# A graph network of two layers in f32 on one core: the second layer's bias put into PSUM by ScalarE ahead of the products instead of by constant products

## The chip, the cores and the metric

The kernel runs on one core of a Trainium2 chip. The metric is the device time of one execution in microseconds; the time before is the median of three runs. A core has TensorE (PE, which multiplies matrices and writes only to PSUM), VectorE (DVE), ScalarE (ACT), GpSimd (POOL), and SyncE (SP), whose queue issues most of the DMAs. Each engine works through its own instruction list in order, and waits on semaphores for the others.

## The reference

`x` has 32 batches of 512 rows (channels) and 1024 columns (nodes). `adj` is 512 by 512. Everything is f32.

```
def L0(x, wq, wk, wm, bm):                 # wm is adj
    q = einsum('c,bcn->bn', wq, x);  k = einsum('c,bcn->bn', wk, x)
    scores = q[:, None, :] + k[:, :, None]
    scores = where(scores > 0, scores, 0.01 * scores)
    att = softmax(scores, axis=-1)
    agg = einsum('bcn,bmn->bcm', x, att)
    return relu(einsum('oc,bcm->bom', wm, agg) + bm[None, :, None])

def L1(x, W, bias):                        # W is adj
    return einsum('bnf,nm->bmf', x, W) + bias      # bias: one value per column

x = layernorm(x + L0(x, wq, wk, adj, bm))          # over the 1024 columns
x = layernorm(x + L1(x, adj, bias))
```

## The kernel before, in words

**Layer 0.** A score depends only on the sum of one q and one k, so the softmax-weighted sums over the nodes can be had from nodes sorted by q and running sums. Per batch the kernel

- loads x (`ld`), forms q and k on PE (`pa`, copied by `pc`; turned by `co`, copied by `cc`), writes q to DRAM as a row (`qw`) and reads it back into all partitions (`ro`, the tile `qb`);
- finds each node's rank by q on DVE (`rk`, eight instructions of 128 by 1024) and the number of partners beyond the leaky unit's bend on ACT (`ct`, eight), closed by `re` and `ce`;
- forms z = adj times x per node on PE. Nodes of the first half come from plain products (`z`, four 128 by 512 tiles, copied by ACT, `zc`); those of the second half from Strassen's seven quarter products (`zU`, `zV`, `zY`, `z11`, `zZ`, `z12`, `z21`, with copies by ACT `zUc`, `zVc`, `zZc`, `zll` and sums on DVE `zup`, `zlr`; operands `x1` to `x4`). The first and the last batches take plain products for all;
- scatters the rows of z to DRAM in sorted order (`sc`, POOL's queue), loads them as a table (`sl`), weights them (`se` on ACT), runs prefix sums up (`u`) and down (`d`) on DVE, closes these across partitions with one-sided triangular products (`cu`, `cd` on PE; ACT's copies `uc`, `te`, `dc`; DVE's additions `tu`, `td`) and writes the table to DRAM (`tw`, and its last row `tl`);
- gathers each node's row (`g`, POOL's queue), forms the weights (`mw`), mixes (`ms` on ACT, `mx` on DVE), transposes back on PE (`t`), adds the residual (`r`, DVE), and normalises (`s0`, `rt`, `rce`, `n0` on ACT).

**Layer 1.** Per batch a product of 512 by 512 with 512 by 1024, again by Strassen's seven products, each in two row groups g = 0, 1 of 128 rows: `U`, `V`, `Y`, `21` gather in a bank `sum`, `11`, `Z`, `12` in a two-bank tile `pair`. adj with 1 added on its diagonal contains the residual. One product is two matmuls of 128 by 128 by 512. DVE makes the operands `t1` to `t4`; ACT copies partial sums out while the bank goes on gathering (`Uc`, `Vc`, `Zc`, `ll`), DVE adds (`up`, `lr`); then the second normalisation (`s1` on ACT, `ra`, `rb`, `r1` on POOL, `n` on ACT) and the store (`st`).

**The bias in layer 1.** Each bank of a sum, and the upper bank of each pair, begins with one row of constants in all its partitions: the sum with the bias of the first 512 columns, the pair with the second half's minus the first's, because Strassen's scheme adds the sum into both halves. A matmul of constants puts it there and opens the group in `quarter` (line 665 in the profile): a 128-row tile `bias_p` of bf16 whose first six rows hold the two halves' bias in three bf16 parts, and a broadcast column `first_0` or `first_10` that selects signs. `bias_parts` makes the rows once at the start.

**PSUM.** Eight banks: pool `p2` has two tiles of two banks (`pair`, the z pairs and the transposes of `t`), pool `p1` has four tiles of one bank under one tag, handed round by the pool: z tiles, `zsum`, `sum`, carries, q and k.

**Order.** The order of the work is written out by hand as lists of words: `head`, `loop` and `tail`. A word is an operation, a batch relative to the list's base, and indices; `emit` issues them in that order, so that each engine's list is the list's words for it in their order. In `loop` batch 0 is in ranking and z, batch -1 in its table, -2 in gathering and mixing, -3 in layer 1. `loop` is run for bases 14 to 18; head and tail write all other batches out.

Of the kernel before, what the change touches and what calls it, by code (L numbers as in the profile page):

```python
# [42 lines left out]
P = 128  # L43
# [6 lines left out]
def adj_resnorm_kernel(  # L50
# [25 lines left out]
    s4 = ctx.enter_context(tc.tile_pool(name="s4", bufs=4))  # L76
    dr = ctx.enter_context(tc.tile_pool(name="dr", bufs=1, space=bass.MemoryType.DRAM))
    p2 = ctx.enter_context(tc.tile_pool(name="p2", bufs=2, space=bass.MemoryType.PSUM))
    p1 = ctx.enter_context(tc.tile_pool(name="p1", bufs=4, space=bass.MemoryType.PSUM))
    ctx.enter_context(tc.manual_schedule())  # L80

# [10 lines left out]
    wqk = const.tile([P, CT, 32], F32, name="wqk")  # L92
# [7 lines left out]
    def adj_load(b):  # L100
        nc.sync.dma_start(out=adj_in, in_=adj.rearrange("(r p) c -> p r c", p=P))

    small = const.tile([P, 16], F32, name="small")
    nbm, eps, power = small[:, 0:4], small[:, 4:5], small[:, 5:9]
    own, spare, inner = small[0:6, 9:14], small[0:1, 14:15], small[:, 15:16]
    room = one.tile([P, NT, 2 * ZR], F32, tag="tab", name="bias_in")[0:6, :, 0:H]
    for h in range(2):
        nc.scalar.dma_start(
            out=room[3 - 3 * h : 6 - 3 * h, 0, :],
            in_=bias[h * H : (h + 1) * H].partition_broadcast(3),  # L110
        )
# [30 lines left out]
    zero = one.tile([P, ZR], F32, tag="end", name="zero")[0:1, :]  # L142
# [15 lines left out]
    bias_p = const.tile([P, H], BF16, name="bias_p")  # L158
    first = const.tile([P, 16], BF16, name="first")
    first_0, first_10 = first[:, 0:1].broadcast_to([P, P]), first[:, 1:2].broadcast_to([P, P])  # L160
    nc.vector.memset(bias_p, 0.0)
    nc.vector.memset(first, 0.0)

    def weights():
        t = p1.tile([P, C], F32, tag="m", name="rows_tp")[:, 0 : 3 * CT]
        nc.tensor.transpose(t, rows, ident[0 : 3 * CT, 0 : 3 * CT])
        nc.vector.tensor_copy(wqk[:, :, 0:2], t[:, 0 : 2 * CT].rearrange("p (r t) -> p t r", r=2))
        nc.vector.tensor_scalar(nbm, t[:, 2 * CT : 3 * CT], -1.0, None, ALU.mult)

    def adj_turn(b):  # L170
        for r in range(CT):
            t = p1.tile([P, CT, P], F32, tag="m", name=f"adj_tp_{r}")
            for c in range(CT):
                nc.tensor.transpose(t[:, c, :], adj_in[:, r, c * P : (c + 1) * P], ident)
            adj_ps.append(t)

    def adj_copy_odd(b):
        for r in range(1, CT, 2):
            nc.scalar.copy(adj_t[:, :, r * P : (r + 1) * P], adj_ps[r])

    def adj_copy_even(b):
        for r in range(0, CT, 2):
            nc.vector.tensor_copy(adj_t[:, :, r * P : (r + 1) * P], adj_ps[r])
        for r in range(CT):
# [16 lines left out]
    def bias_parts(b):  # L201


        i6 = ident[0:6, 0:6]
        nc.vector.tensor_tensor(own[:, 0:3], i6[:, 0:3], i6[:, 3:6], ALU.subtract)
        nc.vector.tensor_reduce(own[:, 3:4], i6[:, 3:6], axis=AX.X, op=ALU.add)
        nc.vector.tensor_scalar(own[:, 4:5], own[:, 3:4], -1.0, None, ALU.mult)
        nc.vector.tensor_copy(first[0:6, 0:1], own[:, 4:5])
        nc.vector.memset(first[0:6, 1:2], 1.0)
        rest, done = room[:, 0, :], room[:, 1, :]  # L210
        for i in range(3):
            part = one.tile([P, 2 * ZR], BF16, tag="end", name=f"bias_part_{i}")[0:6, 0:H]
            nc.vector.tensor_copy(part, rest)
            if i < 2:
                nc.vector.tensor_tensor(rest, rest, part, ALU.subtract)
            if i == 0:
                nc.vector.tensor_scalar(done, part, own[:, 0:1], None, ALU.mult)
            else:
                nc.vector.scalar_tensor_tensor(
                    done, part, own[:, i : i + 1], done, ALU.mult, ALU.add  # L220
                )
        nc.vector.tensor_copy(bias_p[0:6, :], done)
# [18 lines left out]
    def parts(b):  # L241

        s = st[b]
        s.ps = p1.tile([P, C], F32, tag="m", name=f"qk_ps_{b}")[:, 0:Q]
        for c in range(CT):
            for g in range(CT):
                nc.tensor.matmul(  # L247
                    s.ps[32 * g : 32 * g + 32, :], wqk[:, c, :],
# [8 lines left out]
    def cols(b):  # L257
        s = st[b]
        s.ps = p1.tile([P, C], F32, tag="m", name=f"qk_tp_{b}")[:, 0:Q]
# [25 lines left out]
    def top(b):  # L285
        s = st[b]
        settle(b)
        s.ntop = s4.tile([P, 2], F32, tag="top", name=f"top_{b}")
# [4 lines left out]
    def top_end(b):  # L293
# [3 lines left out]
        s.bd = s4.tile([P, 2, NT], F32, tag="bd", name=f"bd_{b}")  # L297
# [3 lines left out]
    def rank(b, j):  # L301
        s = st[b]
        if s.rank is None:
            s.rank = sp.tile([P, NT], F32, tag="rank", name=f"rank_{b}")
        if s.junk is None:
            s.junk = one.tile([P, 4 * ZR], U8, tag="end", name=f"junk_v_{b}")[:, 0:N]
# [11 lines left out]
    def count(b, j):  # L318
        s = st[b]
        if s.sign is None:  # L320
            s.sign = sp.tile([P, NT], F32, tag="sign", name=f"sign_{b}")
# [5 lines left out]
    def count_end(b):  # L327
        s = st[b]
        s.of = s4.tile([P, NT], U32, tag="of", name=f"of_{b}")
# [12 lines left out]
    def product(b, j):  # L342
        s, xt = st[b], xts[b]
        s.z[j] = p1.tile([P, C], F32, tag="m", name=f"z_ps_{b}_{j}")
# [57 lines left out]
    def zU(b):  # L402
        st[b].zsum = p1.tile([P, C], F32, tag="m", name=f"z_sum_ps_{b}")
# [55 lines left out]
    def sums_load(b, h):  # L459
# [4 lines left out]
        if s.tab is None:  # L464
            s.tab = one.tile([P, NT, 2 * ZR], F32, tag="tab", name=f"tab_{b}")
            s.zs = s.tab[:, :, ZR : 2 * ZR]
            s.ac = sp.tile([P, 2, NT], F32, tag="ac", name=f"ac_{b}")
# [14 lines left out]
    def up(b, j):  # L482
# [5 lines left out]
        if j == NT - 1:  # L488
            s.end = one.tile([P, ZR], F32, tag="end", name=f"end_{b}")
            s.up.append(s.end)  # L490
# [793 lines left out]
```

## Time and profile before

| | |
|---|---|
| median of three runs | 1941.6 us (1938.44 to 1947.02) |
| the profiled execution: its time, its span | 1942.71 us, 1940.9 us |
| mean granted clock of TensorE | 0.993 |
| busy: PE, DVE, ACT, POOL | 1887.8, 1704.6, 1483.5, 897.2 us |
| moved by DMA | 558 MB, 288 GB/s on average |
| line 665, constant products | 128 records, 48.4 us busy |

In the profile a line reads: source line, engine, operation, output tile <- input tiles, count, then busy time in all and the mean length in ns of one, then the time that the engine stood idle just before these instructions and what ended most of that. Matmul records overlap: a record runs until its last column has left the array, while the next has long begun. An f32 matmul appears as two records. A wait is put down to what came last.

### The profile page before, as it was taken

To read this page: it belongs to the slowest core of one execution; us is meant where nothing else is said; L and a number is where in the kernel's file an instruction comes from. 1 tells how busy PE (TensorE), PEld (TensorE's weight loads), DVE (VectorE), ACT (ScalarE), POOL (GpSimd) and SP (SyncE) were. 2 spreads that over 40 slices of the span, in tenths; PEclk is the share of its full clock that TensorE was granted. 3 is DMA by queue.
4 is the path that set the end of the run, shared out by engine and by line. 5 is a ranking of instruction groups with operands and counts; after the bars stand their busy time and mean duration, and the time that the engine had idled before them with its cause. 6 is when DMAs were issued, how large, how long until landed. Compare 5 with 4: busy or idle time off the path is not lost.

```text
span 1940.9 us, 23403 instructions
## 1 busy us (share of the span) xinstructions
PE 1887.8 (97%) x7073; PEld 1072.0 (55%) x7073; DVE 1704.6 (88%) x2746; ACT 1483.5 (76%) x2663; POOL 897.2 (46%) x1074
## 2 busy tenths in 40 slices
PE   7988999999999999999999999999999999999897
PEld 3654555555555555566555566555565555554443
DVE  6897899998899889989988989988998989889973
ACT  3566677878778777778787778787777787877786
POOL 5263435335434345454456454455443355445531
PEclk9999999999999999999999999999999999999899
DMA  6577788677888687877787887777888677887862
GB/s 250 197 290 271 286 309 339 253 294 282 313 310 315 252 309 270 331 307 291 290 306 280 317 311 304 277 299 286 308 312 310 262 291 300 308 320 279 331 245 95
DMA packets 147446, 558.05 MB, mean 288 GB/s; under 512 B 19653, under 2 KB 19793, under 8 KB 139129
## 3 DMA queue, kind: packets, MB, share of 16 engines
q1 hardware_dynamic: 89936, 354.40, 48.4%
q0 software_dynamic: 57344, 202.15, 27.6%
q8 instruction: 56, 0.92, 0.2%
q14 instruction: 70, 0.57, 0.1%
q10 hardware_dynamic: 40, 0.02, 0.0%
HBM read 287.08 MB, written 269.42 MB: 287 GB/s over the span
## 4 chain that ended last, share of the span: by engine, by line
PE 78%; DMA 8%; DVE 7%; issue 2%; ACT 2%; POOL 2%; SPq 0%; POOLq 0%; DVEq 0%; ACTq 0%
PE z_ps L346 19%; PE sum_ps L667 18%; PE pair_ps L667 10%; PE z_sum_ps L390 9%; PE z_pair_ps L390 7%; PE pair_ps L702 5%; PE agg_ps L609 4%; DMA table<-tab 3%; PE qk_ps L247 3%; DMA tab<-sorted_z 2%; DVE tab L538 2%; PE carry_ps_True L509 1%; PE carry_ps_False L509 1%; DMA x<-in_x_dram 1%; DMA sorted_z<-zt,to 1%
## 5 line engine op out<-in xcount | busy, mean ns | idle before, releaser
L563 POOL DMA_INDIRECT got<-table,of x256 | 302.3, 1181 | 568.8 <-DMA table<-tab 260.6
L346 PE MATMUL z_ps<-adj_t,x 128*128 128x512 f32 x1088 | 486.9, 594 | 1.4 <-DVE qkc L267 1.1
L451 POOL DMA_INDIRECT sorted_z<-zt,to x256 | 314.0, 1226 | 176.7 <-issue 73.9
L308 DVE SCALAR_TENSOR_TENSOR junk_v<-qb,qkc,tie 128x1024 uint8<-128x1024 f32 x256 | 329.8, 1288 | 10.0 <-DMA qb<-q_row 6.4
L346 PEld LDWEIGHTS z_ps<-adj_t,x 128*128 128x128 f32 x1088 | 202.3, 190 | 225.5 <-issue 212.4
L323 ACT ACTIVATE junk_s<-qb,qkc 128x1024 uint8<-128x1024 f32 x256 | 293.4, 1146 | 19.7 <-DMA qb<-q_row 14.3
L667 PE MATMUL sum_ps<-zt,S 128*128 128x512 f32 x512 | 236.1, 593 | 3.1 <-DVE zt L651 1.4
L585 ACT ACTIVATE got<-got,w 128x512 f32<-128x512 f32 x256 | 172.6, 718 | 42.2 <-DVE w L580 41.8
L590 DVE SCALAR_TENSOR_TENSOR got<-got,w 128x512 f32<-128x512 f32 x256 | 185.6, 746 | 12.0 <-ACT got L585 11.8
L491 DVE SCALAR_TENSOR_TENSOR tab<-tab,ac 128x514 f32<-128x514 f32 x192 | 144.6, 753 | 49.8 <-ACT tab L486 29.2
L617 DVE SCALAR_TENSOR_TENSOR x<-agg_ps,small,x 128x1024 f32<-128x1024 f32 x128 | 163.1, 1280 | 23.9 <-PE agg_ps L609 23.6
L600 ACT ACTIVATE junk<-g,tv 128x1024 uint8<-128x1024 f32 x128 | 146.9, 1148 | 32.9 <-DVE g L722 26.4
L501 DVE SCALAR_TENSOR_TENSOR tab<-tab,ac 128x513 f32<-128x513 f32 x224 | 167.5, 748 | 2.6 <-ACT tab L499 1.9
L667 PEld LDWEIGHTS sum_ps<-zt,S 128*128 128x128 f32 x512 | 96.5, 190 | 121.6 <-issue 105.8
L753 POOL TENSOR_SCALAR tv<-tv 128x1 f32<-128x1 f32 x124 | 53.1, 428 | 238.5 <-ACT junk L600 230.5
L774 ACT ACTIVATE g<-g,nb,tv 128x1024 f32<-128x1024 f32 x124 | 151.0, 1237 | 7.3 <-POOL nb L764 7.2
L600 ACT ACTIVATE junk<-x,tv 128x1024 uint8<-128x1024 f32 x128 | 146.9, 1148 | 12.2 <-DVE x L617 9.9
L538 DVE TENSOR_TENSOR tab<-tab,carry 128x2052 f32<-128x2052 f32 x64 | 146.2, 2291 | 4.7 <-ACT carry L516 4.7
L635 ACT ACTIVATE x<-x,tv 128x1024 f32<-128x1024 f32 x128 | 139.3, 1141 | 0.5
L609 PEld LDWEIGHTS agg_ps<-ident,got 128*128 128x128 f32 x1024 | 116.4, 141 | 36.2 <-issue 24.9
L609 PE MATMUL agg_ps<-ident,got 128*128 128x128 f32 x1024 | 129.4, 274 | 2.7 <-DVE g L722 2.0
L667 PE MATMUL sum_ps<-x,adj 128*128 128x512 f32 x256 | 123.3, 605 | 7.4 <-ACT x L635 7.4
(144 smaller groups left out, 3281.5 us busy)
## 6 DMA issues: line engine op xcount, KB each, us to landing
table<-tab SPq DMA_DIRECT2D x64, 2056.0 KB
tab<-sorted_z SPq DMA_DIRECT2D x64, 1028.0 KB
x<-in_x_dram SPq DMA_DIRECT2D x128, 512.0 KB
out_dram<-g SPq DMA_DIRECT2D x128, 512.0 KB
qb<-q_row SPq DMA_DIRECT2D x32, 512.0 KB
sorted_z<-zt,to POOLq DMA_INDIRECT x256, 5.0
got<-table,of POOLq DMA_INDIRECT x256, 8.0
adj_in<-in_adj_dram SPq DMA_DIRECT2D x1, 1024.0 KB
```

The source lines that it names most:

```text
L308: nc.vector.scalar_tensor_tensor(s.junk, s.qb, s.q[:, j : j + 1], tie[:, at : at + N], ALU.subtract, ALU.is_gt, accum_out=s.rank[:, j : j ...
L323: nc.scalar.activation(junk, s.qb, AF.Sign, bias=s.k[:, j : j + 1], accum_out=s.sign[:, j : j + 1])
L346: nc.tensor.matmul(s.z[j], xt[:, c, j * P : (j + 1) * P], adj_t[:, c, :], start=(c == 0), stop=(c == CT - 1),)
L390: nc.tensor.matmul(ps, a[:, i, k * P : (k + 1) * P], v[:, i, :], start=start and i == 0 and (k == 0 or bank == 1), stop=(i == 1), skip_gro ...
L451: nc.gpsimd.indirect_dma_start(out=sorted_z[b % 2][:, :], out_offset=bass.IndirectOffsetOnAxis(ap=s.to[:, j : j + 1], axis=0), in_=zt[:, j ...
L538: nc.vector.tensor_tensor(v, v, c, ALU.add)
L563: nc.gpsimd.indirect_dma_start(out=s.got[:, j, :], out_offset=None, in_=table[b % 2][:, :], in_offset=bass.IndirectOffsetOnAxis(ap=s.of[:, ...
L585: nc.scalar.activation(down, down, AF.Copy, scale=s.w[:, 1, j : j + 1])
L590: nc.vector.scalar_tensor_tensor(up, up, s.w[:, 0, j : j + 1], down, ALU.mult, ALU.add)
L600: nc.scalar.activation(junk, t, AF.Square, bias=v[0][:, i : i + 1], scale=-float(N), accum_out=v[1][:, i : i + 1],)
L609: nc.tensor.transpose(s.agg[o][:, j * P : (j + 1) * P], s.got[:, j, o * P : (o + 1) * P], ident)
L667: nc.tensor.matmul(ps, a[:, k, g * P : (g + 1) * P], v[:, k, :], start=False, stop=(k == 1), skip_group_check=first is None,)
```

## The change

ScalarE writes the bias into the banks. A tile `seed` holds the 1024 bias values in all partitions (one DMA on SP's queue at the start, and one DVE subtraction that makes the second half relative to the first). `sum_seed` (word `Us`) takes a bank and copies the first half of `seed` into it; `pair_seed` (word `Zs`) copies the second half into the pair's upper bank; the products of `U` and `Z` then add. [...]

`seed` takes 4 KB of each partition. To make room, `rank`, `sign`, `ac`, the first normalisation's statistics and the mixing weights go to single buffers, three others from four to three; the tag `end` is dropped: the last prefix row is written into `tab`'s first row, the totals into `qb`'s buffer, `junk_v` into that of `part`. All three lists are new; `loop` is run for bases 15 to 18.

```diff
+    idle, held, filled = [0, 1, 2, 3], {}, [False] * 4
+    def bank(name, key, keep=False, whole=True, shape=None):
+        want = [i for i in idle if filled[i] == keep] or idle
+        i = want[0]
+        idle.remove(i)
+        held.setdefault(key, []).append(i)
+        t = p1.tile(shape or [P, C], F32, tag=f"m{i}", name=name)
+        was, filled[i] = filled[i], whole
+        return (t, was) if keep else t
+    def release(key):
+        for i in held.pop(key, []):
+            idle.append(i)
...
     def adj_load(b):
         nc.sync.dma_start(out=adj_in, in_=adj.rearrange("(r p) c -> p r c", p=P))
+        nc.sync.dma_start(out=seed, in_=bias.partition_broadcast(P))
...
     def bias_parts(b):
-        nc.vector.tensor_copy(first[0:6, 0:1], own[:, 4:5])
-        nc.vector.memset(first[0:6, 1:2], 1.0)
-        rest, done = room[:, 0, :], room[:, 1, :]
-        for i in range(3):
-            part = one.tile([P, 2 * ZR], BF16, tag="end", name=f"bias_part_{i}")[0:6, 0:H]
-            nc.vector.tensor_copy(part, rest)
...
-        nc.vector.tensor_copy(bias_p[0:6, :], done)
+        nc.vector.tensor_tensor(seed[:, H:N], seed[:, H:N], seed[:, 0:H], ALU.subtract)
...
         if j == NT - 1:
-            s.end = one.tile([P, ZR], F32, tag="end", name=f"end_{b}")
-            s.up.append(s.end)
+            s.up.append(s.tab[:, 0, 0:ZR])
...
     def table_up_end(b):
-        carry_copy([t[0:1, :] for t in st[b].cup], st[b].end[0:1, :])
+        st[b].end = one.tile([P, N], F32, tag="qb", name=f"total_{b}")[0:1, 0:ZR]
+        carry_copy([t[0:1, :] for t in st[b].cup], st[b].end)
...
         for j in range(NT):
-            nc.tensor.transpose(
-                s.agg[o][:, j * P : (j + 1) * P], s.got[:, j, o * P : (o + 1) * P], ident
+            nc.tensor.matmul(
+                s.agg[o][:, j * P : (j + 1) * P], s.got[:, j, o * P : (o + 1) * P], ident,
+                is_transpose=True, start=(j % 4 == 0), stop=True, skip_group_check=True,
             )
...
-    def quarter(ps, a, v, g, first=None):
-        if first is not None:
-            nc.tensor.matmul(ps, first, bias_p, start=True, stop=False)
+    def quarter(ps, a, v, g):
         for k in range(2):
             nc.tensor.matmul(
                 ps, a[:, k, g * P : (g + 1) * P], v[:, k, :], start=False, stop=(k == 1),
...
+    def sum_seed(b, g):
+        s = st[b]
+        s.sum[g], ready = bank(f"sum_ps_{b}_{g}", f"s.{b}.{g}", keep=True)
+        if not ready:
+            nc.tensor.matmul(
+                s.sum[g], none[:, 0:1].broadcast_to([P, P]), none[:, 0:1].broadcast_to([P, H]),
+                start=True, stop=True,
             )
+        nc.scalar.copy(s.sum[g], seed[:, 0:H])
+    def pair_seed(b, g):
+        nc.scalar.copy(pair(b, g)[:, H:N], seed[:, H:N])
...
     def U(b, g):
-        s.sum[g] = p1.tile([P, C], F32, tag="m", name=f"sum_ps_{b}_{g}")
-        quarter(s.sum[g], A11, quarters(b)[0], g, first_0)
+        quarter(s.sum[g], A11, quarters(b)[0], g)
...
     def Z(b, g):
-        quarter(st[b].pair[g][:, H:N], S1, st[b].T1, g, first_10)
+        quarter(st[b].pair[g][:, H:N], S1, st[b].T1, g)
```

A bank is released in `emit` after the word that reads it last (`pc`, `cc`, `zc`, `zll`, `uc` and `te`, `dc`, `ll`). The part of `loop` around the first products of layer 1, before and after:

```
before:
    n0.-3.1 z12.0 g.-2.2 zlr.0 n0.-3.2 t1.-3 U.-3.0 g.-2.5 n0.-3.3 re.0 zup.0 se.-1.0 ct.0.1
    z21.0 sc.0.4 u.-1.0 sc.0.5 11.-3.1 Uc.-3.0 u.-1.1 ct.0.4 t2.-3 g.-2.7 zll.0 11.-3.0 u.-1.2
    se.-1.1 u.-1.3 g.-2.6 V.-3.0 u.-1.4 mw.-2.0 g.-2.4 u.-1.5 ms.-2.2 U.-3.1 Vc.-3.0 u.-1.6
after:
    rk.0.0 sl.-1.1 g.-2.2 zZ.0 rk.0.7 zVc.0 ct.0.6 g.-2.1 tp.-1 zY.0 rk.0.2 zZc.0 Us.-3.0 g.-2.3
    n0.-3.0 z12.0 zlr.0 n0.-3.3 g.-2.5 rk.0.6 se.-1.0 U.-3.0 n0.-3.2 t1.-3 u.-1.0 re.0 zup.0
    z21.0 Uc.-3.0 ct.0.1 u.-1.1 sc.0.4 t2.-3 11.-3.1 zll.0 ct.0.4 u.-1.2 sc.0.5 11.-3.0 Zs.-3.0
    u.-1.3 Us.-3.1 Zs.-3.1 g.-2.4 se.-1.1 V.-3.0 u.-1.4 g.-2.7 mw.-2.0 U.-3.1 u.-1.5 ms.-2.2
```

## The prediction

> **What bounds the kernel now.** I read the page's first part, then the PE groups with shapes kept apart, then the stretch table, then PE's timeline across one batch, and last the waits.
>
> ```profile
> span 1940.9 us, 23403 instructions
> PE 1887.8 (97%) x7073; PEld 1072.0 (55%) x7073; DVE 1704.6 (88%) x2746; ACT 1483.5 (76%) x2663; POOL 897.2 (46%) x1074
> ```
>
> TensorE (PE) is busy for all but 53.1 us. Where those lie is in the stretch table (columns: width, then busy time of PE, PEld, DVE, ACT, POOL, each with its count, then granted clock, DMA share, GB/s):
>
> ```profile
> 0.00:60.00 60.00, 49.45 (x220) 26.13 (x221) 39.33 (x79) 24.42 (x42) 27.69 (x38) 0.97 0.65 227
> ...
> 120.00:180.00 60.00, 48.19 (x164) 26.73 (x163) 49.84 (x83) 37.34 (x71) 28.99 (x33) 0.97 0.65 249
> ...
> 778.00:836.00 58.00, 58.00 (x223) 33.51 (x222) 52.34 (x86) 46.24 (x84) 28.42 (x33) 1.00 0.80 309
> ...
> 1770.00:1830.00 60.00, 55.59 (x170) 26.99 (x168) 55.23 (x87) 45.54 (x85) 29.52 (x30) 0.97 0.92 354
> 1830.00:1890.00 60.00, 51.49 (x148) 24.83 (x148) 49.87 (x81) 51.35 (x88) 29.55 (x35) 0.94 0.70 264
> 1890.00:1940.90 50.90, 38.71 (x111) 18.11 (x109) 20.25 (x34) 32.16 (x57) 5.77 (x16) 0.91 0.23 93
> ```
>
> The start, the fill (120 to 180) and the last 170 us hold 10.6 + 11.8 + 4.4 + 8.5 + 12.2 = 47.5 us of the idle time. In the middle PE is busy without a gap, at full clock. A busy PE need not be at its peak, so I read the repeat length from the chain of waits instead:
>
> ```profile
> 776.35 6.87 PE z_ps L346 x16
> ...
> 834.60 6.87 PE z_ps L346 x16
> ```
>
> The line comes again at 892.83 and 951.07: one batch takes 58.24 us, and the same 16 records take 6.87 us each time: 0.429 us for a 512-column pass, two passes for one f32 product. In a batch DVE needs 52.4 and ACT 46.2 us. So PE sets the pace, DVE is 10% away, ACT 20%.
>
> **The change, part by part.**
>
> *The constant products go.* Their groups:
>
> ```profile
> L665 PE MATMUL pair_ps<-bias_p,first 128*128 128x512 bf16 x64 | 24.2, 379 | 0.0
> L665 PE MATMUL sum_ps<-bias_p,first 128*128 128x512 bf16 x64 | 24.2, 379 | 0.0
> ```
>
> 128 of them, 48.4 us busy. That is not what they cost, because a record's 379 ns contains the pipeline's run-out beneath the next product. The timeline of PE gives start to start:
>
> ```profile
> 806.54 0.38 PE L665 MATMUL sum_ps<-bias_p,first 128*128 128x512 bf16 x1
> 806.75 1.88 PE L667 MATMUL sum_ps<-x,adj 128*128 128x512 f32 x4
> ```
>
> 806.54 to 806.75, and in the chain of waits 0.21 to 0.22 apiece: 0.214 us, half a 0.429 pass. [...] The row is this kernel's own stream, so 27.4. Their weight loads (128 of 98 ns) lie under the pass before and give nothing.
>
> *Some come back.* [...] So 4 x 0.214 = 0.9 us returns. [...]
>
> *What was free already.* Four constant products stand right before a wait of PE and were hidden in it: at 142.48 us (then 4.41 idle), 1796.15 (1.65), 1843.10 (0.45), 1872.13 (0.92). Again 0.9 us that isn't saved.
>
> Net from PE: 27.4 - 0.9 - 0.9 = **25.6 us**, 0.83 a batch: the period should go from 58.24 to 57.4.
>
> *ScalarE's 128 seeds.* No row copies SBUF to PSUM. Nearest by shape are
>
> ```profile
> L585 ACT ACTIVATE got<-got,w 128x512 f32<-128x512 f32 x256 | 172.6, 718 | 42.2 <-DVE w L580 41.8
> ...
> L687 ACT COPY g<-sum_ps 128x512 f32<-128x512 f32 x64 | 36.5, 575 | 24.7 <-PE sum_ps L667 24.6
> ```
>
> SBUF to SBUF with a scale operand 172.6/256 = 0.67 us, from PSUM 36.5/64 = 0.57. I take 0.6: 77 us in all (73 to 86), 2.4 a batch, so ACT goes from 46.2 to 48.6 of 57.4. I put it on the path at nothing in the middle, for this reason (waits of 720 to 1340 us, ten and a half batches: total, times, longest):
>
> ```profile
> ACT zt L352 <- PE z_ps L346: 15.3, 10, 1.8
> ...
> ACT zt L426 <- PE z_pair_ps L390: 12.4, 11, 1.1
> ACT g L693 <- PE sum_ps L667: 12.3, 11, 2.9
> ACT g L687 <- PE sum_ps L667: 11.6, 7, 4.5
> ```
>
> It is ACT that waits for PE, 51.6 us in these four rows, 4.8 a batch; PE has no entry of like size the other way. What is queued behind the seeds: `Us.-3.0` stands before `n0.-3.0`, for which its own product `U.-3.0` waits, and delays it by 0.6. The tightest place is the second sum. Its bank is zsum's, free after `zll.0`. From the end of `z21.0` PE has `11.1`, `11.0` and `V.0`, three of 1.72, 5.2 us, before `U.1`. ACT in that time has the rest of `Uc.0` and `ct.0.1` (0.2 us, since both take 0.57 + 1.27 from the end of `U.0` and `z21.0` runs 1.72), `zll` 0.57, `ct.0.4` 1.27, `Zs.0` and `Us.1` 1.2: 3.2 us. Two us to spare. At the batch's turn `zUc` now follows `ct.7` and two `s0` (3.8 us) and `zV` waits for it; under it lie `z11` 1.72 and `z.0.0` 3.44, again 5.2 against 4.4.
>
> *Other moves, one answer: nothing in the middle.* The last prefix row goes into `tab` where the carry is written later; the totals share `qb`'s buffer, so `qb`'s load also waits for the 2 KB `table_last`. The lists put that write ahead of `qw`, whose own landing `qb` already waited for (issued 828.80, `qb` 830.42: 1.6 us covers it). `junk_v` shares `part` with the carry, behind `td` on DVE's own queue. `rank`, `sign`, `ac`, `r` get one buffer, whose last readers stand earlier in the lists. `ce` moves back to just ahead of the next batch's first `ct`; the gathers that read it on POOL's queue come two batches later, and POOL gets and loses nothing but one queue position of some gathers. At worst the first `ct` waits for a landing; uncovered that is 0 to 1.6 us a batch, below nothing excluded, and I take 0.
>
> *The two ends.* Gone from DVE at the start is the run of bias parts, 37.64 to 43.09 us, for one 128x512 subtraction (0.69, by x_sums L373): 4.8 us of DVE, but PE was busy then. The 512 KB seed load stands on SP ahead of the first `qb`, while that `qb` moves ahead of `ld.1`'s four loads (4 x 0.43 us of issue); the first landing took 7.45 us. Between -5 and +3 for the start. In the tail ACT is at 51.4 of 60 and gets about 3 x 2.4 us more: 0 to +7. The new lists may win or lose waits at both ends that no row prices; I allow 10 us each way and take 0 for all.
>
> *Sum.* The profiled execution took 1942.7 us around its span of 1940.9, 1.1 over the median of 1941.6. 1942.7 - 25.6 = 1917.1; against the median, **1916 us**, 1.3% less.
>
> **The rivals.**
>
> *A: the mechanism as summed, 1916*, 1905 to 1929 with the ends. For it: no gap on PE in the middle, and ACT ahead of PE. 0.74.
>
> *B: ScalarE comes late to a seed, slower.* Place: `Zs.0` and `Us.1` behind `zll.0`, with `U.1` waiting. If ACT arrives 2 us late there, from a late table row at `se` (ACT waited 57.8 us for that load in 27 places, up to 7.8, but only 2.4 in the middle stretch) or from DVE's mixing weights (30.6 us in the middle), both seeds show: 1.2 us of PE idle a batch, 32 x 1.2 = 38, so 1916 + 38 = 1954. It decides from 0.8 us of wait a batch, where it eats the gain. Against it: the 2 us of room and the 4.8 us of waiting for PE that can absorb it. 0.11.
>
> *C: the period stays.* The round from table write to gather, or DVE, holds 58.2 us and the seeds only make PE wait: 1941.6 + 0, say 1939 with the ends. For it: DVE at 52.4, DMA at 80%. Against: PE shows no gap in the middle, and would if another round were the longer one. 0.09.
>
> [...] 0.06, together with losses of this size at the ends.
>
> **How the numbers follow.** About 0.5% (9.7 us, so below 1932 or above 1951) is what a measurement of this kernel can tell from no change. Faster: A's 0.74 and most of D, 0.79. Same: C and the rest, 0.10. Slower: B, 0.11. The predicted time is A's. The range 1904 to 1937 holds A and D and leaves out B, C's most, and a luckier start below.
>
> **What would show it.** Right: no L665 row but 4; copies `sum_ps<-seed` and `pair_ps<-seed`, 128 together, at 0.57 to 0.67 us; the same z_ps line in the chain recurring every 57.4 us; PE busy without gap in the middle stretches; ACT near 1560 us busy, its waits for PE smaller. Wrong: PE rows `sum_ps <- ACT sum_ps` or `z_sum_ps <- ACT zt` with about 1 us each batch (B); a period of 58.2 with PE gaps (C); idle at the ends more than 10 us above 47.5.

## The result: 0.8% slower, and the profile after

The changed kernel takes 1957.18 us (median of five runs, 1956.14 to 1961.67) against 1942.06 for the kernel before (five runs, 1938.44 to 1947.02): a ratio of 1.0084 (1.007 to 1.0098). The prediction had 1916 us and a 0.11 chance of slower. The profiled execution took 1956.8 us around a span of 1955.1. From its page, then its groups:

```profile
span 1955.1 us, 23300 instructions
PE 1876.8 (96%) x6949; PEld 1058.8 (54%) x6949; DVE 1697.8 (87%) x2732; ACT 1543.5 (79%) x2791; POOL 870.5 (45%) x1073
```

```profile
L669 ACT COPY sum_ps<-seed 128x512 f32<-128x512 f32 x64 | 37.6, 587 | 5.8 <-PE sum_ps L665 5.7
L678 ACT COPY pair_ps<-seed 128x512 f32<-128x512 f32 x64 | 37.4, 585 | 25.4 <-PE pair_ps L708 24.8 <-DVE zt L426 0.6
L665 PE MATMUL sum_ps<-none 128*128 128x512 bf16 x4 | 1.8, 442 | 0.0
```

The change does what it says. The constant products are gone but for four zero products (those of `none`, which `sum_seed` runs ahead of a seed where `filled` does not note the bank that `bank` hands it), as forecast, and ScalarE makes 128 seeds of 0.585 us. PE's busy time fell by 11 us, yet its idle time rose from 53.1 to 78.3. The repeat length in the middle, from the chain of waits:

```profile
764.02 6.87 PE sum_ps L656 x16
821.63 6.87 PE sum_ps L656 x16
```

57.61 us, where 58.24 stood before and 57.4 was forecast. The loop got faster. The rest is in the stretch table (same columns as before) and in PE's waits (what waits <- what ended the wait: total, times, longest):

```profile
0.00:60.00 60.00, 49.29 (x219) 25.32 (x220) 36.17 (x66) 25.87 (x44) 30.01 (x38) 0.97 0.67 240
...
120.00:180.00 60.00, 44.80 (x130) 24.37 (x129) 47.13 (x79) 37.83 (x69) 24.62 (x32) 0.86 0.67 262
778.00:836.00 58.00, 58.00 (x222) 33.20 (x221) 52.34 (x86) 48.75 (x89) 27.30 (x36) 1.00 0.80 300
...
1770.00:1830.00 60.00, 53.55 (x142) 25.36 (x142) 48.69 (x71) 45.88 (x86) 22.08 (x31) 0.96 0.84 321
1830.00:1890.00 60.00, 48.47 (x146) 23.49 (x147) 48.91 (x77) 50.73 (x89) 30.37 (x37) 0.94 0.75 274
1890.00:1955.10 65.10, 50.22 (x137) 22.32 (x135) 31.22 (x55) 44.88 (x80) 9.70 (x20) 0.95 0.27 108
```

```profile
PE sum_ps L656 <- ACT sum_ps L669: 10.6, 10, 2.6
...
PE pair_ps L708 <- ACT x L627: 5.8, 3, 4.5
PE carry_ps_False L501 <- ACT part L248: 5.5, 1, 5.5
PE carry_ps_True L501 <- DVE tab L483: 4.5, 1, 4.5
PE agg_ps L600 <- DVE x L609: 4.5, 1, 4.5
```

Two of these waits have a counterpart of the same size in the kernel before:

```profile
PE sum_ps L667 <- ACT x L635: 7.4, 4, 4.4
...
PE carry_ps_True L509 <- DVE end L491: 4.2, 1, 4.2
```

The stretches at the start, in the fill and at the end now hold 10.7 + 15.2 + 6.5 + 11.5 + 14.9 = 58.8 us of PE's idle time, 11.3 more than before. The middle row has no gap. Apart from the first row, the waits shown are mostly long single ones. That first row, ten waits, is PE waiting for seeds of the sums; for seeds of the pairs it waited 1.0 and 0.7 us in two further rows.

**One measure for all the runs.** Busy time hides what a lower clock costs (in the last section the same four records are busy for 2.05 us at a granted clock of 0.50 and for 1.03 without such a period), so I charge every PE record with the distance to the next that its kind shows in an unbroken run (0.429 us for 512 columns of f32, where a record lasts 0.594; 0.215 for bf16, where it lasts 0.379; 1.864 for the 32 records of q and k, and so on), and call the rest of the distance lost. The count runs from PE's first record to its last. Stretches begin and end where the products of a batch's `cu` start. Kernels with "no bias" are explained below.

| | work of PE | lost to batch 2's `cu` | lost from there to batch 28's | lost from there on | lost in all |
|---|---|---|---|---|---|
| before | 1858.2 | 25.0 | 16.3 | 23.0 | 64.3 |
| after | 1831.6 | 35.9 | 30.5 | 39.5 | 105.9 |
| old lists, no bias (e3) | 1830.8 | 25.3 | 16.6 | 24.3 | 66.2 |
| old lists, seeds in gaps (e8) | 1831.8 | 25.3 | 25.5 | 33.7 | 84.5 |
| new lists, no bias (e6) | 1830.8 | 33.2 | 22.4 | 35.2 | 90.8 |
| new head, old rest, no bias (e7) | 1830.8 | 33.2 | 17.1 | 23.3 | 73.6 |
| old head and loop, new tail, no bias (e10) | 1830.8 | 24.4 | 19.9 | 37.2 | 81.5 |

So the change took 26.6 us of work from PE, close to the forecast, and made it lose 41.6 us more. The experiments ask which of the change's three other parts did that: the seeds on ScalarE (theory S), the order of the new lists (L), or the buffers that were joined to make room for the seed (B).

### The profile page after: what moved, and what is told of

Same layout as the page of the kernel before. It is cut to its first block, busy times and chain, and to the rows that moved or that the text cites. A ratio compares the mean times of both kernels' runs of the same rounds, so it can differ in the third digit from the quotient of the medians.

```text
span 1955.1 us, 23300 instructions
## 1 busy us (share of the span) xinstructions
PE 1876.8 (96%) x6949; PEld 1058.8 (54%) x6949; DVE 1697.8 (87%) x2732; ACT 1543.5 (79%) x2791; POOL 870.5 (45%) x1073
## 4 chain that ended last, share of the span: by engine, by line
PE 69%; DMA 13%; ACT 7%; DVE 6%; issue 3%; POOL 2%; SPq 0%; DVEq 0%; POOLq 0%; ACTq 0%
PE sum_ps L656 17%; PE z_ps L339 16%; PE pair_ps L656 9%; PE z_sum_ps L383 7%; PE z_pair_ps L383 5%; DMA table<-tab 5%; PE agg_ps L600 4%; PE pair_ps L708 4%; DMA tab<-sorted_z 4%; PE qk_ps L240 2%; DVE tab L530 2%; DMA sorted_z<-zt,to 2%; PE carry_ps_True L501 1%; PE carry_ps_False L501 1%; ACT junk_s L316 1%
## 5 line engine op out<-in xcount | busy, mean ns | idle before, releaser
L556 POOL DMA_INDIRECT got<-table,of x256 | 293.7, 1147 | 567.6 <-DMA table<-tab 164.2
L444 POOL DMA_INDIRECT sorted_z<-zt,to x256 | 307.0, 1199 | 198.2 <-ACT zt L345 67.2
L301 DVE SCALAR_TENSOR_TENSOR junk_v<-qb,qkc,tie 128x1024 uint8<-128x1024 f32 x256 | 332.0, 1297 | 16.6 <-DMA qb<-q_row 12.6
L483 DVE SCALAR_TENSOR_TENSOR tab<-tab,ac 128x514 f32<-128x514 f32 x224 | 168.6, 752 | 55.9 <-ACT ac L468 37.8
L576 ACT ACTIVATE got<-got,bd 128x512 f32<-128x512 f32 x256 | 174.2, 718 | 38.1 <-DVE bd L571 37.6
L581 DVE SCALAR_TENSOR_TENSOR got<-got,bd 128x512 f32<-128x512 f32 x256 | 183.7, 747 | 7.2 <-ACT got L576 6.7
L609 DVE SCALAR_TENSOR_TENSOR x<-agg_ps,small,x 128x1024 f32<-128x1024 f32 x128 | 162.7, 1280 | 18.4 <-PE agg_ps L600 18.1
L591 ACT ACTIVATE junk<-x,tv 128x1024 uint8<-128x1024 f32 x128 | 146.9, 1147 | 30.5 <-DVE x L609 26.0
L759 POOL TENSOR_SCALAR tv<-tv 128x1 f32<-128x1 f32 x124 | 45.0, 363 | 262.7 <-ACT junk L591 253.1
L656 PE MATMUL sum_ps<-x,adj 128*128 128x512 f32 x256 | 123.1, 604 | 10.7 <-ACT sum_ps L669 10.6
```

What stands on the lines that cost most here:

```text
L301: nc.vector.scalar_tensor_tensor(s.junk, s.qb, s.q[:, j : j + 1], tie[:, at : at + N], ALU.subtract, ALU.is_gt, accum_out=s.rank[:, j : j ...
L444: nc.gpsimd.indirect_dma_start(out=sorted_z[b % 2][:, :], out_offset=bass.IndirectOffsetOnAxis(ap=s.to[:, j : j + 1], axis=0), in_=zt[:, j ...
L556: nc.gpsimd.indirect_dma_start(out=s.got[:, j, :], out_offset=None, in_=table[b % 2][:, :], in_offset=bass.IndirectOffsetOnAxis(ap=s.of[:, ...
L576: nc.scalar.activation(down, down, AF.Copy, scale=s.bd[:, 1, j : j + 1])
L581: nc.vector.scalar_tensor_tensor(up, up, s.bd[:, 0, j : j + 1], down, ALU.mult, ALU.add)
L591: nc.scalar.activation(junk, t, AF.Square, bias=v[0][:, i : i + 1], scale=-float(N), accum_out=v[1][:, i : i + 1],)
```

## The experiments

`bias` is zero in the inputs, so a kernel without it is timed like one with it. For the same reason no run here shows that the products keep a seed other than zero, nor what `filled`, the zero products and the new grouping in `turn` are needed for. Five sessions; in each the kernel before was run too (medians 1943.6 to 1946.2). A difference in us with a sign is of medians against it in the same session, good to some 3 us; the changed kernel's is +15.1.

### Bias away, products back, and the old lists with seeds

**e1: new lists, joined buffers, no bias.** The 128 seeds and the four zero products go, nothing takes their place, and the first products of `U` and `Z` open their sums themselves.

```diff
-        nc.scalar.copy(s.sum[g], seed[:, 0:H])
-        nc.scalar.copy(pair(b, g)[:, H:N], seed[:, H:N])
+                start=(opens and k == 0), stop=(k == 1),      # in U and Z
```

> [...] The bias is left out of the computation. TensorE's work is 1831.6 us as in the changed kernel; only what it waits can differ. Theory S (ScalarE's 75 us of seeds make TensorE wait, for the seeds themselves and for what comes later on ScalarE): the waits fall from 112 us back to about 71, so 1914 to 1925 us. Theory L (the order of the new lists, whatever is in them, costs the waits) and theory B (the buffers that were joined to make room for the seed cost them): 1945 to 1957 us.

Measured 1944.36 us, ratio 1.0004 (0.9993 to 1.0014), +0.4. Without the seeds, and without anything in their place, the new lists are only as fast as the kernel before with all its products. So the seeds cost 14.7 us under these lists; PE's waits for seeds in the changed kernel's trace, 12.3 us in three rows, are nearly of that size. But with nothing in the products' place some 26 us should have been gained, and nothing was: theory S explains half of the miss, and something else the other half.

**e2: the same with constant products in `U` and `Z`.**

```diff
+            nc.tensor.matmul(ps, first.broadcast_to([P, P]), bias_p, start=True, stop=False)
```

> The changed kernel with its lists, its banks and its buffers kept, but with the old kernel's way of opening a sum: a constant product of 512 columns in bf16 inside U and Z, no copy on ScalarE. The constant is zero, so the bias is left out. Against the run without any bias it adds 128 x 0.214 = 27.4 us of TensorE's work. Theory S: 1940 to 1950 us, the time of the kernel before. Theories L and B: 1970 to 1984 us, because new order and buffers keep their waits and the products come on top.

Measured 1962.76 us, 1.0107 (1.0083 to 1.0132), +18.8. It is between the two forecasts: 18.4 over e1 and not 27.4. PE lost 85.0 us here against 98.1 in e1's trace, which is of a run 4.2 us above e1's median; the 9 us that remain are products that ran inside waits. In these lists the seeds are better than the products by 3.7 us, hardly more than the scatter.

**e3: the kernel before, products taken out.**

```diff
-            nc.tensor.matmul(ps, first, bias_p, start=True, stop=False)
+                start=(first is not None and k == 0), stop=(k == 1),
```

> The kernel before with its 128 constant products taken out and nothing in their place (the bias is left out of the computation). This measures the term of the forecast that all theories share: 27.4 us of TensorE's work less, on a path that TensorE bounds. Expected 1912 to 1920 us by all of them. If it comes out above 1930, TensorE's work was not the bound where the products stood, and then the sum of the prediction fails at its first term.

Measured 1917.94 us, 0.9881 (0.9854 to 0.9909), -26.1. The PE term of the forecast is right. Between e1 and e3, which both have no bias, lie 26 us of lists and buffers.

**e4: old lists and old buffers with seeds.**

```diff
-    ct.0.1 z21.0 sc.0.4 ... zll.0 11.-3.0 ... se.-1.1 u.-1.3 g.-2.6 V.-3.0 ...
+    ct.0.1 z21.0 sc.0.4 ... zll.0 Us.-3.1 11.-3.0 ... se.-1.1 u.-1.3 g.-2.6 Zs.-3.0 V.-3.0 ...
```

> The old kernel's three lists and its own buffers for ranks' scratch, totals and small tiles, with the 128 copies on ScalarE in place of the products: each copy is a word set some 0.9 to 2.6 us of TensorE's work ahead of U and of Z, banks handed out as in the changed kernel. The seed is a tile of zeros in bf16, 512 wide, for both halves, so the bias itself is left out. Theory S: the copies cost the same 35 to 45 us of waits here, 1948 to 1962 us. Theories L and B: the old order and the old buffers wait no more than before, 1914 to 1924 us.

Measured 1938.78 us, 0.997 (0.9958 to 0.9982), -5.2: between the theories again. The seeds take back 21 of the 26 us even here. In the loop's own batches they cost nothing (lost between the `cu` of batches 14 and 19: 1.5 us with and without them). They cost where the lists differ from batch to batch: 18.4 against 6.7 us from batch 3 to 14. PE's waits in e4, over the whole span:

```profile
PE pair_ps L660 <- ACT g L722: 5.4, 8, 1.5
...
PE sum_ps L660 <- ACT g L698: 3.3, 2, 2.1
```

These are not seeds but ScalarE's partial-sum copies `Zc` and `Uc`, which stand behind seeds in its queue; in e3 PE waited 0.9 us for such copies. For the seeds themselves it waited 0.8 us in e4 over the whole span. So I set the seeds elsewhere (e8).

### Buffers, and where in the lists

**e5: the changed kernel with two joined buffers apart.** To make room, the seed is a tile of zeros of 1 KB and isn't loaded (not shown below).

```diff
-            s.junk = one.tile([P, 4 * ZR], U8, tag="part", name=f"junk_v_{b}")[:, 0:N]
+            s.junk = one.tile([P, N], U8, tag="junk_v", name=f"junk_v_{b}")
-        st[b].end = one.tile([P, N], F32, tag="qb", name=f"total_{b}")[0:1, 0:ZR]
+        st[b].end = one.tile([P, ZR], F32, tag="end", name=f"total_{b}")[0:1, :]
```

> The changed kernel with its lists and its seeds, but the two joined buffers that the trace shows waits for are taken apart: the ranks' scratch has a tile of its own instead of lying in `part`, and the total row has one instead of lying in `qb`. Room for them comes from the seed, which is a tile of zeros in bf16, 512 wide, for both halves (the copies took 0.585 us from such a tile too), so the bias is left out. Theory B (the joined buffers cost the waits that the new lists show beside the seeds): 27 us less than the changed kernel's 1957, some 1928 to 1936 us. Theory L (the order of the words costs them): only the 5 us at the start can go, 1950 to 1958 us.

Measured 1954.75 us, 1.005 (1.0037 to 1.0063), +9.5. Theory B falls as the main cause: 5.6 us, and 4.8 of them at the start (batch 0's `cu` at 72.0 us, not 76.8). The seed's load is not what they are: e2 has none either, and its first `cu` stands at 76.3.

**e6: new lists, no bias, all of the old buffers.** The edit is e1's with `end`, the double small tiles and an own `junk_v` put back, and the unused seed with its load taken out.

> New lists, no bias and nothing in its place, and all buffers of the kernel before: own `end` tile for the last prefix and the total, small tiles double again, a tile of its own for the ranks' scratch. Only the order of the words and the hand-out of the banks are still the changed kernel's. To be read against 1944 us (new lists, joined buffers, no bias) and 1918 us (old lists, old buffers, no bias). Theory B: 1915 to 1923 us. Theory L: 1938 to 1946 us.

Measured 1941.97 us, 0.9985 (0.997 to 0.9999), -3.3, so 3.7 under e1 and 22.8 over e3. What is left between e6 and e3 is the order of the words, the handing out of banks with its way of grouping the transposes, and at the start the making of the bias rows, which e3 still has. Theory L holds for the most part of it; e7 and e10 keep e6's banks under the old lists and part the two.

**e7: new head, old rest.**

```diff
     emit(head, 0)               # the new one
+    emit(turn_, 15)             # the old loop: zUc.0 first, s0.-3.0 left out
     for b in range(16, 19):
         emit(loop, b)           # the old one
```

> The same buffers and no bias as in the run of the new lists with the old buffers, but only the head list (up to batch 15) is the new one; from there on the old loop and the old tail (the two lists stand at the same words there but for one copy of batch 15 and one square of batch 12, which are put right at the seam). Theory L says the new order loses 11 us in the first three batches, some 3 us from there to batch 14, and the rest in the loop and the tail: 1929 to 1935 us here, and the TensorE of the last four batches waits 24 us as under the old lists. Theory B: 1915 to 1923 us.

Measured 1925.86 us, 0.9902 (0.9874 to 0.993), -19.4. The head costs 6.7 us, and from batch 28 on PE loses 23.3 us, as under the old lists.

**e10: old head and loop, new tail,** e7's counterpart (from another session).

> Old head and old loop, new tail from batch 19 on, no bias, buffers of the kernel before: the counterpart of the run with the new head and the old rest. Theory L, from the waits by stretch: of the 24 us between 1918 and 1942, the head and its fill hold 8, the last three batches 11 to 12, the loop 2, the stretch from batch 19 to 28 about 4: 1931 to 1936 us here. If the loop's own period were what the new lists make worse, this run would stay under 1925 us.

Measured 1934.82 us, 0.9954 (0.9939 to 0.9969), -8.8. The tail costs 17.3 us. Head and tail make 24.0 of the 22.8 between e6 and e3, and the table above shows the losses move with the list: the first column with the head, the last with the tail. Where the old list stands, e7 and e10 lose no more than e3 (23.3 against 24.3, 24.4 against 25.3), so the handing out of banks costs nothing there. The loop's order costs little: between the `cu` of batches 14 and 19 e6 loses 1.6 us more than e3.

### The seeds, taken apart

**e8: old lists, seeds where ScalarE was idle.** The edit is e4's with other places for `Us` and `Zs`.

> Old lists, old buffers and ScalarE's seeds as in the run that gave 1938.8 us, but each seed stands at the place between the freeing of its bank and its use where ScalarE sat idle longest in the trace of the old lists without bias (in 4 of 10 cases there is no such gap of 0.6 us). In the run before, TensorE hardly waited for a seed (0.8 us); it waited for other copies of ScalarE that stood behind one. Theory S (a seed costs what it pushes back on ScalarE): the 21 us over 1917.9 fall by half or more, 1922 to 1930 us. If the seeds cost by ScalarE's load alone, wherever they stand, or by the bank that each takes earlier: 1936 to 1942 us.

Measured 1937.67 us, 0.9962 (0.9948 to 0.9977), -7.6. The better places gained 2.4 us, within the scatter, not the ten expected. Of ScalarE's seeds in e8's trace (idle time of ScalarE just before them, total and times, by what ended it):

```profile
  PE pair_ps L712: 21.0, 25
  PE sum_ps L669: 13.0, 4
```

A gap in ScalarE's trace without seeds is no gap for a seed that has to wait there for PE.

**e9: dead copies.** At e8's words ScalarE copies into its own scratch; nothing waits for it.

```diff
+        junk = one.tile([P, N], U8, tag="junk_s", name=f"junk_d_{b}_{g}")[:, 0:H]
+        nc.scalar.copy(junk, seed)
```

> Old lists, old buffers, no bias: the 128 copies stand on ScalarE at the same words as in the run with the seeds in its gaps, but they write to ScalarE's own scratch in SBUF; no product waits for them, and U takes its bank itself, as late as before. This parts two ways in which the seeds cost 20 us under the old lists. If it is ScalarE's time (each copy pushes back the copies behind it, wherever it stands): as slow as with the seeds, 1932 to 1940 us. If it is what the seeds hold (a product that waits for its seed, a bank taken earlier): 1917 to 1924 us.

Measured 1926.6 us, 0.991 (0.9891 to 0.9929), -17.0.

**e14: dead copies, banks taken as early as for a seed.**

> The run of the old lists with dead copies (1926.6 us), with one thing more: each sum takes its bank at the word at which the seed would be written, not at U. Still no product waits for a copy. Of the 20 us that the seeds cost under the old lists 9 were ScalarE's time; this run parts the other 11. If the bank held longer is what costs (another product finds none free): 1934 to 1939 us. If it is the products that wait for the seed itself or for ScalarE's queue ahead of it: 1925 to 1929 us.

Measured 1925.41 us, 0.9905 (0.9886 to 0.9924), -20.8. The early bank costs nothing. e9 and e14 together put ScalarE's time at 5 to 9 us.

**e17 and e18: half of the seeds real.**

> Old lists, old buffers, 128 copies on ScalarE at the same words as before. The 64 into the sums' banks are real seeds; the 64 for the pairs go to ScalarE's scratch, so that Z opens its own sum and ScalarE does not wait there for the pair's first products. Between 1926 us (all dead) and 1938 us (all real). If the 12 us between them come from the pair seeds (ahead of which ScalarE sat idle for 21 us until a product of the pair had run): 1926 to 1929 us. If they come from the sum seeds: 1935 to 1938 us.

Measured 1930.22 us, 0.9917 (0.9901 to 0.9934), -15.3.

> The counterpart: the 64 seeds of the pairs are real, the 64 of the sums go to ScalarE's scratch and U opens its own sum in a bank taken early. If the pair seeds hold the 12 us: 1935 to 1938 us; if the sum seeds: 1926 to 1929 us; if both by half: 1930 to 1933 us in this run and in its counterpart.

Measured 1931.89 us, 0.9932 (0.9915 to 0.9948), -13.7. Real sum seeds add 3.6 us and real pair seeds 5.2 to the mean of e9 and e14, as forecast for the case that both matter. 7 for ScalarE's time, 3.6 and 5.2 make 16 of e8's 18.5 us over e3; the 2.5 left over are within the scatter. What the real seeds have and the dead ones lack is a wait at each side, ScalarE for PE and PE for ScalarE. Which of the two it is was not parted.

### The new tail's largest wait, in four tries

In e6, as in the changed kernel, PE's longest wait in the tail is 5.5 us ahead of batch 29's lower carry (`cd`). From e6's timeline:

```profile
1750.99 1.75 DVE L531 TENSOR_TENSOR tab<-tab 128x1539 f32<-128x1539 f32 x1
...
1754.60 2.29 DVE L531 TENSOR_TENSOR tab<-tab 128x2052 f32<-128x2052 f32 x1
...
1757.65 0.35 ACT L248 COPY part<-qk_ps 128x256 f32<-128x256 f32 x1
...
1758.00 0.75 DVE L494 SCALAR_TENSOR_TENSOR tab<-tab,ac 128x513 f32<-128x513 f32 x1
...
1758.85 2.05 PE L502 MATMUL carry_ps_False<-tab,behind 128*128 128x257 f32 x4 [5.53 <-ACT part L248]
```

The profile names ScalarE's copy of batch 31's q and k, which stands behind a row of batch 30's counts (1.15 us each) and holds a bank. But the last prefix step on VectorE ends at 1758.75, nearer still to the end of the wait.

**e12: the copy alone moved up, in the whole changed kernel.**

```diff
-    uc.-3 rb.-5.1 mx.-4.6 ct.-2.6 ... s1.-5.2 r.-4.2 pc.-1 ra.-5.2
+    uc.-3 pc.-1 rb.-5.1 mx.-4.6 ct.-2.6 ... s1.-5.2 r.-4.2 ra.-5.2
```

> The changed kernel whole, bias and seeds included, with one word of its tail moved up: batch 31's copy of the query row stands ahead of batch 30's counts on ScalarE (the total's copy can't go with it here, because it lies in the tile that the counts still read). Theory L: 5 us less than 1957, some 1950 to 1953 us. If the joined buffers take the gain back (the copy goes to `part`, in which batch 30's ranks write their scratch): 1955 to 1958 us.

Measured 1961.35 us, 1.0083 (1.0067 to 1.01), +17.8: no gain, and above both forecasts.

**e11: that copy and the total's, without bias and with the old buffers.**

> New lists, no bias, buffers of the kernel before (1942 us), with two words of the tail moved up by 20 and by some 30 places: batch 31's copy of the query row and batch 29's copy of the total now stand ahead of batch 30's counts on ScalarE, as in the old tail, where they stand behind them in the new. In the trace TensorE waits 5.5 us at 1753 us for that copy, since it holds the last bank. Theory L says that such single places, not the lists as a whole, hold the cost: 5 to 6 us less, 1935 to 1938 us. If the wait only moves to the next word that ScalarE serves late (the counts themselves, which the ranks of the batch need): 1940 to 1943 us.

Measured 1937.47 us, 0.9962 (0.9948 to 0.9976), -6.1. The number is close to the forecast and the reason isn't: the wait is still there, under another name, and the stretch between the two `cu` there loses 7.6 us instead of 8.5. The rest of the 2.8 us lies in stretches whose words are the same.

```profile
PE carry_ps_False L502 <- ACT junk_s L316: 5.5, 1, 5.5
```

**e13 and e15: VectorE's words moved instead**, in the tail two prefix steps ahead of the table additions, in the head two residuals ahead of the carry additions; e13 without bias, e15 the whole changed kernel.

```diff
-    t.0.2 td.1.0 t.0.0 td.1.1 tw.1.0 r.0.2 tw.1.1 tl.1 r.0.0
+    t.0.2 r.0.2 td.1.0 t.0.0 r.0.0 td.1.1 tw.1.0 tw.1.1 tl.1
-    uc.-3 ... r1.-5.1 tu.-3.0 t.-4.3 ... d.-3.1 ct.-2.3 tu.-3.1 ... d.-3.0
+    uc.-3 ... r1.-5.1 d.-3.1 d.-3.0 tu.-3.0 t.-4.3 ... ct.-2.3 tu.-3.1 ...
```

> New lists, no bias, buffers of the kernel before (1942 us), with four words moved at two places where TensorE waits 4.5 and 5.5 us. In the head, the residuals of two rows of batch 0 go ahead of the two carry additions of batch 1's table (2.27 us each on VectorE); in the tail, the last two prefix steps of batch 29 go ahead of the two table additions that stand in front of them (1.75 and 2.29 us). The run with the query row's copy moved left the 5.5 us wait where it was, so the copy that the profile names is not what it waits for. Theory V (the new order sets VectorE's long table additions in front of the short result that TensorE needs): both waits go, 8 to 10 us less, 1932 to 1936 us. If the waits have another cause again: 1939 to 1943 us, with the two lines still there.

Measured 1941.75 us, 0.9983 (0.9971 to 0.9995), -4.5.

> The changed kernel whole, with bias, seeds and joined buffers, and the same four words moved as in the run without bias. Theory V: 8 to 10 us less than 1957, 1946 to 1950 us: still not faster than the kernel before. If ScalarE's seeds or the joined buffers wait at the same places anyway: 1952 to 1958 us.

Measured 1960.29 us, 1.0073 (1.0057 to 1.009), +14.1. Theory V fails in both. In e13's tail 4.7 us of the 5.5 are left, and in the head the wait for the residual shrank from 4.5 to 2.8 while the next, for a normalised row, grew from 4.5 to 5.9:

```profile
PE pair_ps L705 <- ACT x L629: 5.9, 1, 5.9
PE agg_ps L602 <- DVE x L611: 2.8, 2, 2.3
```

**e16: both moves in the tail.**

> New lists, no bias, buffers of the kernel before, new head as it is; in the tail both moves together: batch 31's query row and batch 29's total ahead of batch 30's counts on ScalarE, and batch 29's last two prefix steps ahead of the two table additions on VectorE. Each move alone left TensorE's wait of about 5 us ahead of batch 29's lower carry in place (5.5 and 4.7 us). If the wait is the later of two that end together, it is gone with both: the stretch from batch 29's upper carry to batch 30's loses 3 to 4 us instead of 8, and the time is 1935 to 1938 us. If a third thing ends there too, the stretch keeps its 8 us, and the time stays at 1939 to 1943 us: then the tail is a matter of its order as a whole, not of single words.

Measured 1938.76 us, 0.9964 (0.9948 to 0.9981), -6.8. The wait ahead of the carry is gone, so two had ended together there. A third takes its place after it, again behind the counts on ScalarE, now the carry's own copy:

```profile
PE z_ps L339 <- ACT carry L509: 3.5, 1, 3.5
```

The stretch loses 6.3 us (8.5 in e6, 0.8 in e3). Both answers that were written down are half right: two waits ended together, and the order as a whole is at fault. In the old tail batch 30's counts are done before batch 29's `cu`; in the new they stand in the middle of batch 29's carries.

## Why the prediction was wrong, step by step

- **Constant products, -25.6 us: right.** e3 shows -26.1, and PE's work fell by 26.6 in the changed kernel. The row's 0.214 us a product holds: 26.1 over 128 is 0.204, with four of the products hidden in waits. For the 0.9 us of four zero products in the sum no run shows the term: before has none of them, and no run takes them out alone. The count was right: the changed kernel's trace has four L665 records, three of 0.379 us and, in a stretch at a granted clock of 0.50 (160 to 164 us), one of 0.631.
- **"ScalarE's 128 seeds ... on the path at nothing in the middle": nearly right for the loop, wrong as a sum.** The duration (0.6 forecast, 0.585 measured) fits, and so nearly does the 57.4 us period: 57.61, against 57.37 in e1, so 0.24 a batch for the seeds. But the loop is run for four batches only, and head and tail write out the rest; there the tight places differ from batch to batch. The seeds cost 14.7 us in the new lists and 18.5 in the old. Only 0 to 7 us had been allowed, for the tail.
- **"The new lists may win or lose waits at both ends that no row prices; I allow 10 us each way and take 0 for all": the step that turned the sign.** The term was put at 0 and bounded by 10. The order alone costs 22.8 us; measured apart, the head costs 6.7 and the tail 17.3. Loop periods say nothing of this, and the instruction order, which could be read beforehand, was followed only in the loop.
- **"Other moves, one answer: nothing in the middle": off by 4 to 6 us,** most of it at the start, for which up to +3 had been allowed. `junk_v` in `part` was cleared for the loop, where it stands behind `td`; in the head the next batch's `pc` waits for batch 0's ranks instead (in the changed kernel's trace 5.0 us of ScalarE and 2.65 of PE).
- **Rival B (1954) had the number by luck.** It set 1.2 us on every batch. The period rose by 0.2 over the forecast, and PE's waits for seeds are 12.3 us in all, not 38.
- **C and D fall:** the period shortened, and the zero products, which D had ahead of every sum (1929), are four. Of the signs named ahead, the last one came true: idle at the ends 11.3 us above 47.5, with the bound at 10.

The account against the kernel before: -26.1 products, +22.8 order, +3.7 joined buffers, +14.7 seeds, which is the +15.1 measured. It closes by construction, since each part is the difference of two neighbouring runs; taken in another order, with the old lists first, the seeds are 18.5.

No version that computes the bias is faster than the kernel before. e4 and e8 are 0.3 to 0.4% faster than before, but their seed is a tile of zeros of 1 KB; a real one takes 4 KB, and making that room is what joined the buffers. The old lists with a real seed on joined buffers weren't run, so whether the change could win with the old order stays open.

## What to carry to other kernels

Work taken off the engine that bounds a steady loop can be lost again at the two ends, here when their order changed with it (26.6 us of PE's work went, 41.6 more were lost in waits and at a lower clock); price head and tail batch by batch, or keep the old lists and change nothing else. A helper engine's spare time in the loop was not spare time where the lists are irregular: copies that wait for the busy engine and are waited for (0.590 us each in e8) cost 18.5 us here, dead ones of nearly the same length (0.617 in e17) 7. And where the profile names one releaser at a long wait, look for what else ends within a microsecond of it before moving a word (in e6 the copy ends 0.85 us and the prefix step 0.10 us ahead of the wait's end).

## What the hardware showed that I had not expected

Some waits of PE went with a lower granted clock in the microseconds around their end, and the products there took longer. The same products after the tail's wait (e6) and without it (e16), from their timelines:

```profile
1758.85 2.05 PE L502 MATMUL carry_ps_False<-tab,behind 128*128 128x257 f32 x4 [5.53 <-ACT part L248]
...
1761.21 4.86 PE L339 MATMUL z_ps<-adj_t,x 128*128 128x512 f32 x8
```

```profile
1751.22 1.03 PE L502 MATMUL carry_ps_False<-tab,behind 128*128 128x257 f32 x4
...
1752.31 3.60 PE L339 MATMUL z_ps<-adj_t,x 128*128 128x512 f32 x8
```

The carry's four records take twice as long (2.05 us against 1.03) and the next eight 1.26 us more; the granted clock is 0.50 from 1756.91 to 1763.74 us in e6 and 1.00 after that, and so 0.92 between the two `cu`, against 1.00 in e3. The changed kernel has this wait too, of 5.54 us up to 1770.62, and a granted clock of 0.50 from 1768.02 to 1774.84. A shorter wait stands ahead of such a period as well: in the changed kernel PE waits 2.65 us at 32.8 us for the copy behind batch 0's ranks, and the 24 records after it take 12.16 us, against 10.47 in e6, where the buffer is its own and the wait is gone. The granted clock is 0.50 from 34.05 to 37.46 us.

```profile
32.84 0.44 PE L255 MATMUL qk_tp<-ident,part 128*128 128x128 f32 x2 [2.65 <-ACT part L248]
33.12 12.16 PE L339 MATMUL z_ps<-adj_t,x 128*128 128x512 f32 x24
```

But another wait of 2.65 us in the same trace, up to 1806.89, has none: the granted clock is 1.00 from 1774.84 to 1843.11. The length of a wait alone does not tell whether the clock falls; what does was not shown. The fill shows the clock most: 0.97 before, 0.86 after. In periods at 0.50 PE was busy for 27.3 us in the changed kernel and 15.0 before; if the products there take twice as long, as the carry's did, half of the 12.3 us between them, some 6 of the 41.6 us, are by estimate the clock's. By that estimate waits at the ends cost more here than the waits view sums up.
